# Query groups of 8, 10, 10, 10 and 10 rows in place of six of 8, with the key stacks in a ring of three thirds

## The chip, the cores and the metric

The kernel runs on one core of a Trainium2 chip. The metric is the time of one execution on the device in microseconds (us), as the median of several runs. Before the change it is 2807.74 us, the median of 3 runs that took 2807.44 to 2809.26.

## The reference

The input is four images (B = 4) of 384 channels (C) and 48 x 48 = 2304 tokens (N). There are eight heads of 48 channels. Inputs and outputs are float32. Cut to what matters:

```python
local = depthwise_conv_7x7(x) * bn_scale + bn_shift        # per channel
q, k, v = split_heads(layernorm(x) @ qkv_w.T + qkv_b)       # layernorm over channels
q = q + split_heads(layernorm(local))
attn = softmax(q @ k.T * 48 ** -0.5)
out = x + (attn @ v) @ proj_w.T + proj_b
```

So each image has two kinds of work: a convolution of 49 taps on each of 384 channels, which feeds the queries only, and attention of 2304 queries over 2304 keys in each of eight heads.

## The kernel before

**Tiling.** Channels lie on the 128 partitions in three chunks (`CC = 3`); tokens lie along the free dimension. An image is cut into `NG = 6` groups of `RG = 8` rows, that is `G = 384` columns. The same groups serve the queries, the keys, the values and the output projection. `NT = B * NG = 24` query groups are numbered `t = (b, g)`. Keys come in `KB = 18` blocks of 128. The eight heads form `NP = 4` pairs, and the two heads of a pair take the two halves of the partitions (the two row halves of the TensorE array).

**A slot.** The work of one query group is 12 slots (`NSLOT`): pair `s // 3`, and a third of the keys `s % 3`, which is `BATCH = 6` key blocks. Slot `s` first computes scores for its six blocks (`score_batch`, then `score`), and then weighs the values with them (`weigh_batch`, then `weigh`). For each block, `score` issues six matmuls with weights of 64 x 128 and 384 columns: three terms (high and low parts of queries and keys, stacked in `qs` and `ks`) times two row halves, in `float32r`, which takes one pass. They go to the two banks of a PSUM tile. One exponential on ScalarE takes the 768 columns to a tile `pt` in SBUF (a ring of 5 buffers). `weigh` issues two float32 matmuls per block, with weights of 128 x 64, one per head; each runs as two passes on the array, so that the profile counts four records. The 64 columns of a head's weights are its 48 values, a column of ones that sums the softmax's denominator, and 15 columns whose sums aren't read. At the end of the slot `sums_out` copies the sums out on ScalarE, and `sums_add` adds thirds on VectorE. The exponential is taken without subtracting a maximum first; `inside` keeps a flag of whether the denominators stayed in a safe range, and a second pass that subtracts it runs only if they did not, which the data here never ask for.

**Stacks of keys.** For an image, the stacks of all four pairs are written to DRAM (`wide`) by many small transfers in the keys' stage (`keys_out`, on GpSimd's queue, called POOL in the profile). Pair 0's is built in SBUF (through `stack_head` on SyncE's queue, SP) and kept in DRAM by `keep_stack` (one store of 2304 KB in slot 1 of the image's first group). During attention the pairs alternate in two SBUF buffers of a whole pair (tag `ks`, `bufs=2`). In each slot, `load_keys` issues the load of a third (768 KB) of the next pair.

**The convolution.** VectorE does it for group `t + 1` while TensorE works on group `t`: one `scalar_tensor_tensor` per tap and chunk (line 289), with a first `tensor_scalar` (285). For group 0 and group 1 some taps of chunk 0 (`PE_TAPS = 10` and `MORE_TAPS = 18`) run on TensorE, with diagonal weights (`products`). `load_slab` brings the rows of a group with three more on each side.

**What sets the order.** On TensorE, VectorE and ScalarE the instructions run in the order in which they are written. SP's and POOL's are placed by the framework's scheduler. Where convolution instructions go is decided by `plan`: each point of the program (two per slot, five per step of the keys' stage) has a `spare` time, each group's convolution a due point, and `convolve` takes the share of a point from one stream. In image 0 (`early`) the norm of the next group's local queries goes through TensorE: `mean_kept` multiplies by a matrix of means, first at slot `norm_slots(t)[0]`, which is 8 for group 0 and 7 for the others, and again a slot later. Then `centre`, `local_end` and `query_end` form the queries, and `high_queries` (ScalarE) and `low_queries` (VectorE, then small transfers within `qs` on SP) their stack. In later images these norms go through transfers instead (`following`).

**Between images** stands a keys' stage of six steps. Each step projects values, keys and queries of a group of the new image, and the output of a group of the old image (`fetch` of the attention held in DRAM, `load_residual`, `finish`); each is three matmuls of 384 columns per chunk (line 529, two passes each). The last group's output is not held, but read from SBUF.

```python
            score_batch(t, s)
            if s == 0:
                gather_tails(*reversed(queries[t]))
            if pair < NP - 1 or g < NG - 1:
                load_keys(b, (pair + 1) % NP, third)
            if s == 1 and g == 0:
                keep_stack(b)
```

Of the kernel before, what the change touches and what calls it, by code (L numbers as in the profile page):

```python
# [23 lines left out]
RG = 8  # L24
BATCH = 6
# [21 lines left out]
def unshifted_pass(  # L47
# [28 lines left out]
    NT = B * NG  # L76
    PAD = KS // 2

# [18 lines left out]

    xn = {}

    def place_x(b, g):  # L100
        xn[b, g] = big.tile([P, CC, G], F32, tag=f"xn{g}", name=f"xn{b}_{g}")
        return xn[b, g]
# [6 lines left out]
    def load_slab(b, g, parts=1, queue=nc.gpsimd):  # L109
        first, end = max(0, g * RG - PAD), min(H, (g + 1) * RG + PAD)  # L110
        t = work.tile([P, CC, (RG + 2 * PAD) * W], F32, tag="slab", name=f"slab{b}_{g}")

        edges = (first, (g + 1) * RG, end) if parts == 2 else (first, end)
        for a, e in zip(edges, edges[1:]):
            load_packed(t[:, :, (a - first) * W : (e - first) * W], x[b, :, a * W : e * W], queue)
        slabs[b, g] = (t, first, end)
# [11 lines left out]
    natural = work.tile([P, G], F32, tag="qt", name="natural", bufs=1)[:, 0 : CC * (T0 + 1)]  # L128
# [21 lines left out]
    start_up = big.tile([P, 2, N], F32, tag="ks", name="start_up", bufs=2).rearrange("p a n -> p (a n)")  # L150
# [58 lines left out]
    def pack():  # L209
# [19 lines left out]
        work.tile([P, 2, C], F32, tag="pt", name="pt", bufs=5) for _ in range(-(-PE_TAPS // 6))  # L229
    ]  # L230
    staged = [piece(CC, C) for _ in range(3)]
# [18 lines left out]
    def window(slab, a, g, first, end, c, tap):  # L250

        dy, dx = tap // KS - PAD, tap % KS - PAD
        r0, r1 = max(g * RG, -dy), min((g + 1) * RG, H - dy)
        c0, c1 = max(0, -dx), min(W, W - dx)
        if r0 >= r1:
            return None
        img = slab[:, c, : (end - first) * W].rearrange("p (h w) -> p h w", w=W)
        a = a.rearrange("p (h w) -> p h w", w=W)
        return (
            img[:, r0 + dy - first : r1 + dy - first, c0 + dx : c1 + dx],  # L260
            a[:, r0 - g * RG : r1 - g * RG, c0:c1],
        )

    def conv_ops(t):
        b, g = divmod(t, NG)
        if t + 1 < NT:
            load_slab(*divmod(t + 1, NG))
        slab, first, end = slabs[b, g]
        acc = work.tile([P, CC, G], F32, tag="acc", name=f"acc{t}", bufs=3)
# [29 lines left out]
    def products(g, n, diagonal):  # L299
        total = two_banks()[:, 0, :G]  # L300
# [11 lines left out]
    def make_more():  # L312
        for tag, bufs in (("qs", 5), ("qs", 5)):
            d = work.tile([P, CC, G], F32, tag=tag, name="more", bufs=bufs)
# [9 lines left out]
    def norm_slots(t):  # L324
        return (8 - (t > 0), None) if t + 1 < NG else (5, 8)

    def spare(t, s, half):
        b, g = divmod(t, NG)
        first, second = norm_slots(t)
        time = 3.6 - (0.0 if half else 0.6) - (0.6 if half and s % 3 == 1 else 0.0)  # L330
        if b + 1 < B and g >= later(b + 1):
# [5 lines left out]
        if t + 1 < NG:  # L337
# [3 lines left out]
        elif g < NG - 1:  # L341
# [3 lines left out]
        return max(0.3, time)  # L345

    def later(b):

        return X_LATER + (b == 1)

# [12 lines left out]
    for t in range(NT):  # L363
        if t % NG == 0 and t:
            points += [("kv", t, g, h) for g in range(NG) for h in range(5)]
            room += [spare_at_keys(t // NG, g, h) for g in range(NG) for h in range(5)]
# [3 lines left out]
    due = []  # L370
    for t in range(1, NT):
        last = ("slot", t - 1, norm_slots(t - 1)[0] - (t >= NG), t < NG) if t % NG else ("kv", t, 4, 0)
        due.append((points.index(last), t * each - MORE_TAPS))
    share = {}

    def plan(done):

        done = float(done)
        given = round(done)
        for i, point in enumerate(points):  # L380
            ahead = [(sum(room[i:end]), n - done) for end, n in due if end > i]
            rate = max((n / time for time, n in ahead[: 2 * NG]), default=0.0)
            done += rate * room[i]
            share[point] = round(done) - given
            given = round(done)
# [6 lines left out]
    few = G // 32  # L392

    def spread(s):

        return s.rearrange("p (k i) -> p k i", i=1).to_broadcast([P, few, 32])

    class Norm:
# [8 lines left out]
        def __init__(self, src):  # L407
            self.src = src
            self.buf = work.tile([P, CC, G], F32, tag="sq", name="sq")

        def squares(self, at=slice(0, G)):
# [20 lines left out]
        def mean(self, m=None):  # L432
            self.m = two_banks()[:, 0, :G] if m is None else m
            nc.tensor.matmul(self.m, lhsT=mean_w, rhs=self.buf[:, 0, :], start=True, stop=True)

        def mean_by_chunk(self, src, m=None):
            self.m = two_banks()[:, 0, :G] if m is None else m
            project(self.m, lambda c: mean_w, lambda c: src[:, c, :])

        def mean_kept(self, src):  # L440

            m = two_banks()[:, 0, :G]
# [9 lines left out]
        def centre(self, raw=None, at=slice(0, G)):  # L452
# [5 lines left out]
        def root(self, at=slice(0, G)):  # L458
# [6 lines left out]
        def newton(self, at=slice(0, G)):  # L465
# [7 lines left out]
        def out(self):  # L473

            part = work.tile([P, few], F32, tag="part", name="part")
            parts = dram.tile([32, 4, few], F32, tag="parts", name="parts")
            self.four = work.tile([P, 4 * few], F32, tag="four", name="four")
# [12 lines left out]
        def few_in(self):  # L490
            self.v = work.tile([P, few], F32, tag="few", name="few")
            nc.vector.tensor_reduce(
                self.v, self.four.rearrange("p (q k) -> p k q", k=few), AX.X, ALU.add
# [14 lines left out]
        def few_root(self):  # L508
            self.y = work.tile([P, few], F32, tag="few_y", name="few_y")
            self.u = work.tile([P, few], F32, tag="few_u", name="few_u")  # L510
# [11 lines left out]
        def scale(self, rs, at=slice(0, G)):  # L522
# [16 lines left out]
    values = {}  # L539
    lows = deque()  # L540
# [3 lines left out]
    def place_keys(b, p):  # L544
        stacks[b, p] = big.tile([P, 2, N], HALF, tag="ks", name=f"ks{b}_{p}", bufs=2)
        return stacks[b, p].bitcast(F32)
# [9 lines left out]
    def keys_out(b, g, u, k):  # L556
        at = slice(g * G, (g + 1) * G)
        k = k.bitcast(F32)
        if g == u == 0:
            place_keys(b, 0)  # L560
            for p in range(1, NP):
                wide[b, p] = dram.tile([P, 2, N], F32, tag=f"wide{p}", name=f"wide{b}_{p}")
        for j in range(2):
            if u == 0:
                stack_head(stacks[b, 0].bitcast(F32)[:, :, at], j, k, nc.sync)
# [12 lines left out]
    def keep_stack(b):  # L578
        wide[b, 0] = dram.tile([P, 2, N], F32, tag="wide0", name=f"wide{b}_0")
        nc.gpsimd.dma_start(out=wide[b, 0], in_=stacks[b, 0].bitcast(F32))  # L580

    def load_keys(b, p, i):
        at = slice(i * BATCH * P, (i + 1) * BATCH * P)
        if i == 0:
            place_keys(b, p)
        nc.gpsimd.dma_start(out=stacks[b, p].bitcast(F32)[:, :, at], in_=wide[b, p][:, :, at])  # L586

    def from_x(b, g, before=None, ao=None):
# [3 lines left out]
        flat = big.tile([P, NB * NH * HA + 64 - HA], F32, tag=f"v{g}", name=f"v{b}_{g}")  # L592
        v = flat[:, 0 : NB * NH * HA].rearrange("p (t h d) -> p t h d", t=NB, h=NH)
        values[b, g] = flat
        nc.gpsimd.memset(v[:, :, :, HD:HA], 1.0)
        nc.gpsimd.memset(flat[:, NB * NH * HA :], 0.0)
# [12 lines left out]
        def key(u, r):  # L609
# [3 lines left out]
            k = work.tile([P, 2, G], HALF, tag="pt", name=f"k{b}_{g}_{u}", bufs=5)  # L613
# [22 lines left out]
        def output(co, r):  # L636
            project(r[:, :G], lambda c: w_o[:, c, co * P : (co + 1) * P], lambda c: ao[:, c, :])
            yield
            finish(before, co, r[:, :G])
# [28 lines left out]
    row = work.tile([P, CC, G], F32, tag="rb", name="row", bufs=1)[:, 0]  # L668
# [85 lines left out]
    def query_end(t):  # L754

        acc = accs.pop(t)
        q = xn[divmod(t, NG)]
        q3 = work.tile([P, G], F32, tag="qt", name=f"qt{t}", bufs=1)
# [12 lines left out]
    def high_queries(t, p):  # L771
        qs = work.tile([P, 3, G], HALF, tag="qs", name=f"qs{t}_{p}", bufs=5)
# [22 lines left out]
    def sums_out():  # L795
# [3 lines left out]
        t, p, i, sums = ended.pop()  # L799
        if i:  # L800
            part = work.tile([P, G], F32, tag="part_o", name=f"o{t}_{p}_{i}")
            nc.scalar.copy(part[0 : 64 + HA], sums[0 : 64 + HA, 0, :G])  # L802
            parts_of.append((t, p, i, part))
            return
        if p == 0:
            ao = work.tile([P, CC, G], F32, tag="ao", name=f"ao{t}")
            ao3 = work.tile([P, G], F32, tag="aot", name=f"aot{t}", bufs=1)
            den = dram.tile([NH, G], F32, tag="den", name=f"den{t}")
# [3 lines left out]
        nc.scalar.copy(dst[0 : 64 + HA], sums[0 : 64 + HA, 0, :G])  # L812
# [21 lines left out]
    def divide(t):  # L834

        few = NH * G // P
        rd = work.tile([P, few], F32, tag="rd", name="rd")
        rb = work.tile([P, CC, G], F32, tag="rb", name="rb", bufs=1)
        rden = dram.tile([NH, G], F32, tag="rden", name=f"rden{t}")
# [3 lines left out]
        for bound, op in ((SAFE, ALU.is_le), (1 / SAFE, ALU.is_ge)):  # L843
            nc.vector.scalar_tensor_tensor(inside, rd, bound, inside, op, ALU.mult)
        nc.sync.dma_start(out=rden.rearrange("h (k f) -> (h k) f", f=few), in_=rd)
        heads = rden[0:6].rearrange("(c h) n -> h c n", h=2)
        for j in range(2):
# [3 lines left out]
                out=rb[r : r + HD], in_=heads[j : j + 1].to_broadcast([HD, CC, G])  # L851
            )
            nc.sync.dma_start(out=rb[r + HD : r + 64], in_=last.to_broadcast([16, CC, G]))
# [4 lines left out]
    def load_residual(t, tag="qs", bufs=5):  # L858
        b, g = divmod(t, NG)
        xr = work.tile([P, CC, G], F32, tag=tag, name=f"xr{t}", bufs=bufs)  # L860
        nc.gpsimd.dma_start(
            out=xr, in_=x[b, :, g * G : (g + 1) * G].rearrange("(c p) n -> p c n", p=P)
        )
        residuals[t] = xr
# [3 lines left out]
    def hold(t):  # L868
        held[t] = dram.tile([P, CC, G], F32, tag=f"held{t % NG}", name=f"held{t}", bufs=1)
        nc.gpsimd.dma_start(out=held[t], in_=outputs[t][0])  # L870

    def fetch(t):
        if t < NT - NG:
            ao = work.tile([P, CC, G], F32, tag="qs", name=f"af{t}", bufs=5)
        else:
            ao = big.tile([P, CC, G], F32, tag=f"xn{t % NG}", name=f"af{t}")
# [903 lines left out]
```

## Time and profile before

| | |
|---|---|
| median of 3 runs | 2807.74 us (2807.44 to 2809.26) |
| the profiled execution | 2808.18 us |
| its span in the profile | 2806.1 us |
| what lies around the span | 2.1 us |
| granted TensorE clock, mean | 0.995 of full speed |
| attention of image 0 starts at | 169.8 us |
| a query group's 12 slots, mostly | 88.3 us |
| query groups 0, 1, 2 of image 0 | 93.7, 100.2, 93.7 us |
| keys' stages between images | 144.5, 143.5, 140.1 us |
| the last slot ends at | 2765 us |

The engines are PE (TensorE's matmuls), PEld (its loads of weights), DVE (VectorE), ACT (ScalarE), POOL (GpSimd) and SP (SyncE). A profiled line of a group of instructions names the line in the kernel, the engine, the operation, output <- inputs, and the shapes. In the windows view each engine has its busy time and, in brackets, its number of instructions; then come the granted clock, the busy share of the DMA engines and what they moved in GB/s. A busy time says how much an engine had to do, not whether anyone waited for it: for that the chain of work that ended last and the waits are read.

### The profile page before, as it was taken

Reading aid. Unit: us, or ns where it says so; the run is one execution under the profiler, and the core shown is the slowest. Engines: PE = TensorE matmul, PEld = TensorE weight load, DVE = VectorE, ACT = ScalarE, POOL = GpSimd, SP = SyncE. Lnnn points to the kernel's source line nnn. Section 1 sums busy time; section 2 is a strip of 40 time slices with the busy share of each in tenths; the row PEclk is TensorE's granted clock in tenths of the full one; section 3 lists DMA queues with packets and bytes.
Section 4 is the critical chain, followed back from the end, with each engine's and each line's share of the span. In section 5 each row is a group of like instructions: output and inputs, shape, how many; then the busy total and the mean of one; then the engine's idle time right before and its main releaser. Section 6 shows DMA issues by size and latency. Waiting matters only on the chain.

```text
span 2806.1 us, 53985 instructions
## 1 busy us (share of the span) xinstructions
PE 2773.0 (99%) x19330; PEld 1747.7 (62%) x19330; DVE 2430.9 (87%) x4801; ACT 1648.4 (59%) x2659; POOL 729.7 (26%) x1353
## 2 busy tenths in 40 slices
PE   9999999999999999999999999999999999999999
PEld 6565666666655666666655566666665566666665
DVE  6879999988999999999888999998988999998402
ACT  4356666667424766677632566777662266666762
POOL 5731111111374111111156311111117711111110
PEclk9999999999999999999999999999999999999999
DMA  7354545455455455545545544455445554554542
GB/s 139 98 143 131 154 136 147 146 157 161 105 155 164 127 161 146 159 154 166 156 118 146 171 144 151 142 167 173 138 122 148 142 167 147 155 175 152 170 143 72
DMA packets 180919, 410.35 MB, mean 146 GB/s; under 512 B 67776, under 2 KB 122240, under 8 KB 180128
## 3 DMA queue, kind: packets, MB, share of 16 engines
q0 software_dynamic: 84736, 325.45, 37.0%
q1 hardware_dynamic: 92912, 77.73, 12.0%
q8 instruction: 155, 2.54, 0.4%
q10 hardware_dynamic: 2992, 3.62, 0.4%
q14 instruction: 124, 1.02, 0.1%
HBM read 298.25 MB, written 64.73 MB: 129 GB/s over the span
## 4 chain that ended last, share of the span: by engine, by line
PE 87%; DVE 6%; DMA 3%; POOL 1%; issue 1%; ACT 1%; SPq 0%; DVEq 0%; ACTq 0%; POOLq 0%
PE o L917 39%; PE r L902 33%; PE r L529 14%; DVE acc L289 3%; DMA qs<-qs 1%; PE r L304 1%; DMA parts<-part 1%; DMA wide<-k 1%; POOL wide L554 0%; DMA four<-parts 0%; DVE k L617 0%; DMA ks<-k 0%; DMA rd<-den 0%; DVE xn L761 0%; DVE xr L883 0%
## 5 line engine op out<-in xcount | busy, mean ns | idle before, releaser
L289 DVE SCALAR_TENSOR_TENSOR acc<-slab,vec,acc 128x368 f32<-128x368 f32 (+7 forms) x3430 | 1762.5, 586 | 2.2
L910 ACT ACTIVATE pt<-r 128x768 f32<-128x768 f32 x1728 | 1247.8, 827 | 104.0 <-PE r L902 68.4
L917 PE MATMUL o<-pt,v 128*64 128x384 f32 x6912 | 1178.3, 490 | 0.0
L902 PEld LDWEIGHTS r<-qs,ks 64*128 64x128 f32 x10368 | 898.2, 186 | 197.2 <-issue 178.2
L902 PE MATMUL r<-qs,ks 64*128 64x384 f32 x10368 | 995.4, 341 | 20.3 <-DMA qs<-qs 9.1
L917 PEld LDWEIGHTS o<-pt,v 128*64 128x64 f32 x6912 | 470.9, 137 | 586.8 <-issue 507.2
L586 POOL DMA_DIRECT2D ks<-wide x276 | 200.1, 727 | 1025.6 <-PE r L902 976.4
L802 ACT COPY o<-o 113x384 f32<-113x384 f32 x192 | 92.4, 481 | 402.5 <-PE o L917 402.5
L529 PE MATMUL r<-xn,w_qk 128*128 128x384 f32 x864 | 283.7, 486 | 0.0
L529 PEld LDWEIGHTS r<-xn,w_qk 128*128 128x128 f32 x864 | 164.2, 190 | 114.5
L529 PE MATMUL r<-w_v,xn 128*128 128x384 f32 x432 | 144.9, 488 | 0.0
L606 ACT COPY v<-r 128x384 f32<-128x384 f32 x72 | 32.1, 481 | 186.9 <-PE r L529 186.9
L821 DVE TENSOR_TENSOR ao<-ao,o 113x384 f32<-113x384 f32 x144 | 79.8, 554 | 66.9 <-ACT o L802 66.3
L529 PE MATMUL r<-af,w_o 128*128 128x384 f32 x360 | 119.1, 487 | 0.0
L529 PEld LDWEIGHTS r<-w_v,xn 128*128 128x128 f32 x432 | 81.4, 190 | 58.6 <-issue 2.4
L812 ACT COPY ao<-o 113x384 f32<-113x384 f32 x72 | 34.6, 481 | 139.7 <-PE o L917 139.7
L95 POOL DMA_DIRECT2D slab<-in_x_dram x92 | 55.6, 613 | 222.6 <-DVE acc L289 216.7
L529 PEld LDWEIGHTS r<-af,w_o 128*128 128x128 f32 x360 | 68.2, 190 | 47.8 <-issue 0.6
L554 POOL DMA_DIRECT2D wide<-k x192 | 96.3, 506 | 5.4 <-issue 5.0
L95 POOL DMA_DIRECT2D xn<-in_x_dram x72 | 39.5, 557 | 212.5 <-DVE qs L779 212.5
L576 POOL DMA_DIRECT2D wide<-k x192 | 92.7, 488 | 6.8 <-issue 2.6
L570 POOL DMA_DIRECT2D wide<-k x144 | 71.1, 496 | 83.1 <-ACT k L614 61.3
(136 smaller groups left out, 1302.1 us busy)
## 6 DMA issues: line engine op xcount, KB each, us to landing
ks<-wide POOLq DMA_DIRECT2D x276, 768.0 KB, 6.5
qs<-qs SPq DMA_DIRECT2D x528, 48.0 KB
xr<-in_x_dram POOLq DMA_DIRECT2D x24, 576.0 KB, 5.8
slab<-in_x_dram POOLq DMA_DIRECT2D x32, 378.0 KB, 6.6
wide<-k POOLq DMA_DIRECT2D x480, 24.0 KB, 1.9
held<-ao POOLq DMA_DIRECT2D x20, 576.0 KB, 3.3
af<-held POOLq DMA_DIRECT2D x20, 576.0 KB, 5.1
rb<-rden SPq DMA_DIRECT2D x48, 216.0 KB
```

The source lines that it names most:

```text
L95: queue.dma_start(out=dst[p0 : p0 + piece.shape[0]], in_=piece)
L289: nc.vector.scalar_tensor_tensor(dst, src, weight, dst, ALU.mult, ALU.add)
L529: nc.tensor.matmul(dst, lhsT=weights(c), rhs=src(c), start=c == 0, stop=c == CC - 1)
L554: queue.dma_start(out=dst[r + 32 * i : r + 32 * i + 32, 1], in_=k[r + 16 : r + HD, 1])
L570: nc.gpsimd.dma_start(out=last[16 * u : 16 * u + 16, 0], in_=k[r : r + 16, 0])
L576: nc.gpsimd.dma_start(out=last[to : to + 16, 1], in_=k[r : r + 16, 1])
L586: nc.gpsimd.dma_start(out=stacks[b, p].bitcast(F32)[:, :, at], in_=wide[b, p][:, :, at])
L802: nc.scalar.copy(part[0 : 64 + HA], sums[0 : 64 + HA, 0, :G])
L821: nc.vector.tensor_add(dst, dst, part[0 : 64 + HA])
L902: nc.tensor.matmul(r[:, j, :G], lhsT=ks[rows, w, kb * P : (kb + 1) * P], rhs=qs[rows, m, :], start=i == 0, stop=i == 2,)
L910: nc.scalar.activation(pt, r[:, :, :G], AF.Exp, scale=SCALE)
L917: nc.tensor.matmul(sums[halves[j], 0, :G], lhsT=values[t // NG, kb // NB][:, first : first + 64], rhs=pt[:, j, :], start=i == 0, stop=i == ...
```

## The change

The rows of an image are cut twice. The queries, their convolution and norms go in five groups, of 8, 10, 10, 10 and 10 rows (`ROWS`, `NA = 5`), which is one of 384 columns and four of 480 (`GM`); `NT` becomes 20, and `tokens[g]` is a group's slice of the columns. Keys, values and the projections of the keys' stage stay in six groups of 384 columns. The output projection has pieces of its own (`pieces_out`): four of 384, one of 288 and one of 480 columns, of which the last is the last query group.

What follows from it in the buffers:

- x lies in one SBUF tile (`whole`) instead of six, the values in one (`every_value`) instead of six, and the held attention of an image in one DRAM tile. Groups are slices of these.
- The key stacks lie in a ring of three buffers that each have a third of a pair, instead of two that have a whole pair. `load_keys(b, n)` loads the third of slot `n = s + 2`, one per slot. `keep_stack` stores thirds, the first two in the keys' stage (steps 3 and 5), the third in slot 0.
- `pt` has 4 buffers instead of 5. Tiles of a query group are made for 480 columns (`qs`, `acc`, `sq`, `ao` and so on). The weights that are prepared at the start lie in `qs` tiles meanwhile.
- `plan` weighs the convolution by columns. Norms, `divide` and DRAM tiles take the size of their group. `begins(b)` is the query group in which the next image's x starts to be normalized.

The diff, cut to its core:

```diff
+ROWS = 8, 10, 10, 10, 10
...
+    NA = len(ROWS)
+    NT = B * NA
+    GM = max(ROWS) * W
+    row_of = [sum(ROWS[:g]) for g in range(NA + 1)]
+    tokens = [slice(row_of[g] * W, row_of[g + 1] * W) for g in range(NA)]
+    pieces_out = [slice(i * G, min((i + 1) * G, tokens[-1].start)) for i in range(NG - 1)]
+    pieces_out.append(tokens[-1])
...
+    whole = big.tile([P, CC, N], F32, tag="xn", name="xn")
...
-        xn[b, g] = big.tile([P, CC, G], F32, tag=f"xn{g}", name=f"xn{b}_{g}")
+        xn[b, g] = whole[:, :, g * G : (g + 1) * G]
...
-        return max(0.3, time)
+        return max(0.3, time) * columns_of(t) / G
...
+    def begins(b):
+
+        return NA - NG + later(b)
...
-        last = ("slot", t - 1, norm_slots(t - 1)[0] - (t >= NG), t < NG) if t % NG else ("kv", t, 4, 0)
-        due.append((points.index(last), t * each - MORE_TAPS))
+        last = ("slot", t - 1, norm_slots(t - 1)[0] - (t >= NA), t < NA) if t % NA else ("kv", t, 4, 0)
+        counts.append(t * each - MORE_TAPS)
+        weights.append(weights[-1] + (counts[-1] - counts[-2]) * columns_of(t) / G)
+        due.append((points.index(last), weights[-1]))
...
+    every_value = big.tile([P, KB * NH * HA + 64 - HA], F32, tag="v", name="v")
...
-    def place_keys(b, p):
-        stacks[b, p] = big.tile([P, 2, N], HALF, tag="ks", name=f"ks{b}_{p}", bufs=2)
-        return stacks[b, p].bitcast(F32)
+    def place_keys(b, p, i):
+        stacks[b, p, i] = big.tile([P, 2, third], HALF, tag="ks", name=f"ks{b}_{p}_{i}", bufs=3)
+        return stacks[b, p, i].bitcast(F32)
...
-    def keep_stack(b):
-        wide[b, 0] = dram.tile([P, 2, N], F32, tag="wide0", name=f"wide{b}_0")
-        nc.gpsimd.dma_start(out=wide[b, 0], in_=stacks[b, 0].bitcast(F32))
-
-    def load_keys(b, p, i):
-        at = slice(i * BATCH * P, (i + 1) * BATCH * P)
-        if i == 0:
-            place_keys(b, p)
-        nc.gpsimd.dma_start(out=stacks[b, p].bitcast(F32)[:, :, at], in_=wide[b, p][:, :, at])
+    def keep_stack(b, i):
+        at = slice(i * third, (i + 1) * third)
+        nc.gpsimd.dma_start(out=wide[b, 0][:, :, at], in_=stacks[b, 0, i].bitcast(F32))
+
+    def load_keys(b, n):
+        p, i = n // 3 % NP, n % 3
+        at = slice(i * third, (i + 1) * third)
+        nc.gpsimd.dma_start(out=place_keys(b, p, i), in_=wide[b, p][:, :, at])
...
         def output(co, r):
-            project(r[:, :G], lambda c: w_o[:, c, co * P : (co + 1) * P], lambda c: ao[:, c, :])
+            n = ao.shape[-1]
+            project(r[:, :n], lambda c: w_o[:, c, co * P : (co + 1) * P], lambda c: ao[:, c, :])
...
-        qs = work.tile([P, 3, G], HALF, tag="qs", name=f"qs{t}_{p}", bufs=5)
+        qs = work.tile([P, 3, GM], HALF, tag="qs", name=f"qs{t}_{p}", bufs=5)
+        qs = qs[:, :, : columns_of(t)]
...
     def score(t, p, kb):
-        ks, qs = stacks[t // NG, p], stacked[t, p]
+        ks, qs = stacks[t // NA, p, kb // BATCH], stacked[t, p]
+        at = slice(kb % BATCH * P, (kb % BATCH + 1) * P)
+        n = columns_of(t)
...
-                    r[:, j, :G],
-                    lhsT=ks[rows, w, kb * P : (kb + 1) * P],
+                    r[:, j, :n],
+                    lhsT=ks[rows, w, at],
...
-        pt = work.tile([P, 2, G], F32, tag="pt", name="pt", bufs=5)
-        nc.scalar.activation(pt, r[:, :, :G], AF.Exp, scale=SCALE)
+        pt = work.tile([P, 2, GM], F32, tag="pt", name="pt", bufs=4)[:, :, :n]
+        nc.scalar.activation(pt, r[:, :, :n], AF.Exp, scale=SCALE)
...
+        if g in (3, 5):
+            keep_stack(0, g // 2 - 1)
...
+                if gk in (3, 5):
+                    keep_stack(b, gk // 2 - 1)
...
-            if pair < NP - 1 or g < NG - 1:
-                load_keys(b, (pair + 1) % NP, third)
-            if s == 1 and g == 0:
-                keep_stack(b)
+            if s == 0 and g == 0:
+                keep_stack(b, 2)
+            if (s or g) and (s < NSLOT - 2 or g < NA - 1):
+                load_keys(b, s + 2)
```

## The prediction

> **What bounds the kernel now.** I read three views in this order: busy times, the chain that ended last, the timeline of one slot. The page first:
>
> ```profile
> PE 2773.0 (99%) x19330; PEld 1747.7 (62%) x19330; DVE 2430.9 (87%) x4801; ACT 1648.4 (59%) x2659; POOL 729.7 (26%) x1353
> ...
> PE 87%; DVE 6%; DMA 3%; POOL 1%; issue 1%; ACT 1%; SPq 0%; DVEq 0%; ACTq 0%; POOLq 0%
> ```
>
> TensorE is busy 99% and carries 87% of the chain, so the change is worth what it does to PE's instruction stream, unless another engine starts to hold PE up. The candidate is VectorE: 87% is a mean, and some stages are fuller. The timeline of PE in one slot (start, length, ..., count):
>
> ```profile
> 2411.89 3.41 PE L902 MATMUL r<-qs,ks 64*128 64x384 f32 x36
> 2415.23 4.09 PE L917 MATMUL o<-pt,v 128*64 128x384 f32 x24
> 2419.25 0.97 PE L902 MATMUL r<-qs,ks 64*128 64x384 f32 x8
> ```
>
> A slot is 36 score matmuls, then 24 records of weighing; the next starts at 2419.25, so it lasts 7.36 us. Between starts the trace shows 173.4 ns for two scores (the two row halves run side by side) and 322.5 ns for a pass of weighing over both column halves. 18 x 173.4 + 12 x 322.5 = 6991 ns; the other 367 ns are the seams: +108 before the first score, +112 from score to weigh, +50 at the first weigh, +97 back. Twelve slots make 88.3 us, and most groups take 88.3.
>
> Groups 0 to 4 of image 0 are longer, because there PE computes the next group's norm means and needs its convolution finished. By stage (core 0: PE, PEld, DVE, ACT, POOL busy):
>
> ```profile
> 169.80:263.50 93.70, 92.96 (x734) 58.64 (x733) 82.81 (x154) 62.98 (x96) 14.99 (x24) 1.00 0.49 147
> 263.50:363.70 100.20, 95.35 (x736) 60.50 (x734) 92.38 (x179) 63.07 (x96) 14.00 (x21) 0.98 0.48 140
> 363.70:457.40 93.70, 92.95 (x736) 58.64 (x734) 91.20 (x177) 62.64 (x96) 14.05 (x21) 1.00 0.50 145
> ```
>
> DVE is at 91.20 of 93.70 in the third. In the first it was idle for 9.77 us at the start (to 178.16, behind ACT's copy of qs) and then ran without a gap:
>
> ```profile
> 227.78 7.61 DVE L289 SCALAR_TENSOR_TENSOR acc<-slab,vec,acc 128x376 f32<-128x376 f32 x12
> 235.31 0.47 DVE L285 TENSOR_SCALAR acc<-slab,vec 128x384 f32<-128x384 f32 x1
> 235.96 2.20 PE L529 MATMUL r<-acc,mean_w 128*128 128x384 f32 x6
> ```
>
> conv(1) ends at about 235.3, and PE comes to its mean at 235.96: 0.7 us of slack. This is where larger groups will hurt.
>
> **What the Trainium skill says.** "TensorE: Matmul & The Clock Gate", section "Back-to-back issue gap", gives N/2.4 + 2.5 ns for a single matmul. Two column halves of 384 make 322.5, as the trace has it; for scores it would be 162.5, the trace has 173.4, so their extra 10.9 ns follows another rule. The same page, "LDWEIGHTS (loading the stationary operand)", gives P/1.2: 107 ns for 128 columns and 53 for 64; the seams of 108 and 50 agree. A seam costs one exposed weight load, whatever the columns. "PSUM — Partial Sum Buffer", "The four PSUM rules": one output may have 512 fp32 columns; 480 fits, but no run here shows it yet. "VectorE: DVE Perf Modes", "The TRN2 errata — SBUF-src ops pay a fixed extra latency per instruction", says a cost fixed per instruction: convolution starts are 364 ns apart at 225 columns and 529 at 384, that is 129 ns + 1.04 per column.
>
> **The change, part by part.**
>
> *Slots of 480 columns.* Each interval grows by 96/2.4 = 40 ns per column half: scores 213.4 (the 13.4 beyond 160 kept), weighing 402.5, seams unchanged. 18 x 213.4 + 12 x 402.5 + 367 = 9038 ns, against 1.25 x 7358 = 9198 for the same columns. An image goes from 6 x 88.3 = 529.8 to 88.3 + 4 x 108.46 = 522.1 us; four images: **-30.6**. Of it -17.6 is 48 slots' seams, -11.6 are scores, -1.4 weighing. Extra columns in an existing instruction were never seen, so I bound the scores: strictly proportional (216.7 ns) gives back 11.6; if the 10.9 ns stand for weight loads that 480 columns cover, a pair takes 202.9 and 3456 pairs gain 10.5 ns each, 36 more.
>
> *Norm means on PE in image 0*: five times +5.45 become four times two means of 6 x 402.5 ns and 1.6 of waits, 6.4: **-1.6**.
>
> *Products of group 1*: 18 taps x 2 passes x 92 columns x 0.83 ns = **+2.8**.
>
> *VectorE in group 0.* Group 0 keeps 384 columns, so PE arrives at the mean as early as before, while conv(1) now has 480. After the gap at 178 there are 98 of its instructions, each 0.096 to 0.10 us longer: 9.4 to 9.8 us. Slack was 0.7, so PE waits about **+9** in slot 8 (conv ops move with the planner's weights, but the due point is the same). In group 1 PE lost 6.35 us in the first slot to late qs transfers. If that recurs, DVE catches up and the net is +9.4; if it goes, DVE is 3.5 short at the next mean, net +6.5. I take **+8**. Later DVE gains: its instruction grows by 629/529 = 1.19 while PE's group grows by 1.23 to 1.25, 3430 convolution instructions become 2854.
>
> *Ring of three thirds.* 276 key loads become 228, issued one per slot instead of three per pair. A load waits for the scores of the slot before, and has two slots and most of a score phase, 2 x 9.04 + 5 = 23 us, to land:
>
> ```profile
> ks<-wide POOLq DMA_DIRECT2D x276, 768.0 KB, 6.5
> ```
>
> "DMA: Bandwidth & Descriptors", "Anatomy of one DMA", would give 2.0 + 786/436 = 3.8 us as an estimate; the trace's 6.5 decides. So 16 us of cover: 0. SP issues 440 qs loads for 528, in the same slots. It also breaks up bursts: in group 8 one slot took 12.01 us because three loads released together ran ahead of a qs transfer, so I take **-3** (0 to -4.65). The keep of pair 0 becomes three stores, two of them in the keys' stage on POOL's queue before stack pieces: 8 more issues of 0.56 us; POOL has about 15.7 of 23 us per step there, so 0, at worst +3.4 over three boundaries.
>
> *Image boundaries.* PE idles about 5 us there for the first qs. The output projection now has 288 columns in the fifth and 480 in the last piece, so the last query chain starts 1.44 us earlier under the same PE work: up to -4.3 for three, **-2** taken. Tail +0.4.
>
> *pt ring 5 to 4.* The fifth and sixth exp of a slot now wait for its first two weighings. At 0.85 us each (0.691 now), the sixth ends 7.0 us into the slot and is needed at 8.1: covered by 1.1 us; if not, every slot would lengthen. One tile for x and one for values: waits go by region in the changed program, 0. One held tile per image, read in pieces that straddle groups: each fetch follows its stores by whole groups, 0.
>
> Sum: -30.6 - 1.6 + 2.8 + 8 - 3 - 2 + 0.4 = **-26**. The profiled execution took 2808.18 (span 2806.1 and 2.1 around it), 0.4 above the median of 2807.74. That gives **2782**, with the terms' bounds 2773 to 2796.
>
> **Rivals.**
>
> *Scores proportional to columns* (12%): no seam inside, +11.6, 2794. Against it stands 322.5 = 2 x 160 + 2.5 for weighing, where the constant is small.
>
> *Scores set by weight loads* (9%): the slot is 8.85 us or less, about 2746. For it: each pair needs two loads of 128 columns, and weighing, with loads of 64, has no such extra. Against: short matmuls with one such load each start 112 ns apart, far under 173.4, and the two row halves' loads overlap.
>
> *VectorE bounds more of image 0* (10%): if the planner's shares put convolution later in groups 1 to 3 too, three more waits of 5 to 6 us: 2800. For it: 91.20 of 93.70. Against: DVE's 1.19 against PE's 1.23.
>
> *The ring comes late* (9%, the slower side). POOL issues in order, and behind a wait every key load is held:
>
> ```profile
> POOL ks L586 <- PE r L902: 976.4, 77, 26.3
> POOL slab L95 <- DVE acc L289: 216.7, 19, 24.6
> POOL xn L95 <- DVE qs L779: 212.5, 18, 18.1
> ```
>
> (total, times, longest, us.) A wait of 24.6 that begins just after a load holds the next one 24.6 - 9.0, then come 2.2 of slab issues and 6.5 to land: 24.3, 1.3 beyond the 23. With 37 x 20/24 = 31 such waits it decides from 26/31 = 0.84 us each; at 1.3 each the time is 2822. Against it: the waits before mostly end before the loads behind them are due, since they start with the burst; a single load per slot lets them sit closer to their release.
>
> That the change doesn't do what it says is unlikely: instruction counts of the changed program are 8640 scores and 2880 weighings against 10368 and 3456.
>
> **The numbers.** Likeliest case 60%: 2782. A measurement tells 0.2% (5.6 us) from no change: faster is under 2802.1, slower over 2813.4. Cases below: main, proportional, weight loads and most of VectorE: 0.84 faster; rest of VectorE and mild ring delays 0.07; ring 0.09. The range reaches from between the main case and the weight-load case, 2764, to the VectorE case, 2802.
>
> **What will show it.** Slots of 9.04 us (9.20: proportional; 8.85: weight loads); score pairs 213 ns apart; in group 0 about 9 us of PE idle ahead of the mean, released by DVE's convolution; key loads landed before their scores, no wait of PE on ks; a smaller share of DVE later. It would be wrong if PE's waits on ks or pt appear in many slots, or if DVE's waits go beyond group 1.

## The result and the profile after

The changed kernel takes 2783.61 us (median of 4 runs, 2782.53 to 2784.88) against 2808.50 for the kernel before (4 runs): a ratio of 0.991, with a 95% interval of 0.9893 to 0.9927. That is faster by 24.9 us; the prediction was 2782. The profiled execution took 2782.53 us with a span of 2780.7, which is 25.4 us less than the span before.

The page of the changed kernel, busy times and the chain by engine:

```profile
PE 2749.9 (99%) x16438; PEld 1555.9 (56%) x16438; DVE 2339.9 (84%) x4082; ACT 1639.0 (59%) x2281; POOL 696.2 (25%) x1273
...
PE 87%; DVE 5%; POOL 4%; DMA 2%; issue 1%; ACT 1%; SPq 0%; DVEq 0%; ACTq 0%; POOLq 0%
```

PE still sets the time (99% busy, 87% of the chain), with 23 us less of busy time. DVE's share fell from 87 to 84%. One slot of 480 columns in the timeline of PE (start, length, line, form, count):

```profile
2413.57 4.16 PE L952 MATMUL r<-qs,ks 64*128 64x480 f32 x36
2417.66 5.05 PE L967 MATMUL o<-pt,v 128*64 128x480 f32 x24
2422.64 0.70 PE L952 MATMUL r<-qs,ks 64*128 64x480 f32 x4
```

From 2413.57 to 2422.64 are 9.07 us. The first three query groups of image 0, in the windows view (length, then busy PE, PEld, DVE, ACT and POOL, granted clock, DMA share, GB/s):

```profile
171.50:278.00 106.50, 97.20 (x733) 59.61 (x732) 91.44 (x146) 64.91 (x96) 13.29 (x20) 0.95 0.43 121
278.00:396.40 118.40, 115.29 (x736) 61.38 (x734) 116.07 (x190) 77.27 (x96) 14.31 (x21) 1.00 0.43 123
396.40:511.80 115.40, 114.68 (x736) 61.37 (x734) 109.92 (x181) 77.35 (x96) 14.28 (x21) 1.00 0.45 124
```

Group 0 has the 384 columns it had before, yet takes 106.5 us instead of 93.7. PE is busy for only 97.20 of it, and its clock is 0.95. The timelines of VectorE and PE around the mean show why:

```profile
237.03 9.51 DVE L307 SCALAR_TENSOR_TENSOR acc<-slab,vec,acc 128x480 f32<-128x480 f32 x13
246.46 0.55 DVE L868 TENSOR_TENSOR ao<-ao,o 113x384 f32<-113x384 f32 x1
```

```profile
234.80 4.09 PE L967 MATMUL o<-pt,v 128*64 128x384 f32 x24
246.69 5.14 PE L568 MATMUL r<-acc,mean_w 128*128 128x480 f32 x6 [7.80 <-DVE acc L307]
```

VectorE works without a gap until the convolution of group 1 ends at about 246.5; PE is done with its slot at 238.9 and waits 7.80 us. The six matmuls that follow take 5.14 us, where the same six take 2.68 in the next group (at 353.63).

From the two traces, stage by stage, the 25.4 us are made up as follows (after minus before, us):

| part | predicted | found |
|---|---|---|
| slots: 192 of 9.075 and 48 of 7.378, for 288 of 7.357 | -30.6 | -22.3 |
| norm means on PE in image 0: 4 x 6.4 for 5 x 5.45 | -1.6 | -1.6 |
| products of group 1, start of the attention 169.8 to 171.5 | +2.8 | +1.7 |
| VectorE and the qs wait in groups 0 and 1 | +8 | +8.2 |
| group 8's long slot | -3 | -4.65 |
| three image boundaries | -2 | -6.0 |
| tail | +0.4 | -0.7 |
| sum | -26 | -25.35 |

The sum agrees with the span, so nothing large is missing. The slots brought 8.3 us less than predicted, and the boundaries, group 8, the start and the tail together 7.8 us more.

### The profile page after: what moved, and what is told of

It is laid out like the page before. It is cut to its first block, busy times and chain, and to the rows that moved or that the text cites. A ratio compares the mean times of both kernels' runs of the same rounds, so it can differ in the third digit from the quotient of the medians.

```text
span 2780.7 us, 46399 instructions
## 1 busy us (share of the span) xinstructions
PE 2749.9 (99%) x16438; PEld 1555.9 (56%) x16438; DVE 2339.9 (84%) x4082; ACT 1639.0 (59%) x2281; POOL 696.2 (25%) x1273
## 3 DMA queue, kind: packets, MB, share of 16 engines
q1 hardware_dynamic: 83072, 77.72, 12.2%
## 4 chain that ended last, share of the span: by engine, by line
PE 87%; DVE 5%; POOL 4%; DMA 2%; issue 1%; ACT 1%; SPq 0%; DVEq 0%; ACTq 0%; POOLq 0%
PE o L967 40%; PE r L952 32%; PE r L568 14%; DVE acc L307 4%; POOL wide L594 1%; DMA wide<-k 1%; DMA slab<-in_x_dram 1%; POOL wide L619 1%; POOL wide L592 1%; POOL wide L591 0%; POOL wide L613 0%; DVE k L661 0%; PE r L322 0%; DMA qs<-qs 0%; PE r L1010 0%
## 5 line engine op out<-in xcount | busy, mean ns | idle before, releaser
L307 DVE SCALAR_TENSOR_TENSOR acc<-slab,vec,acc 128x450 f32<-128x450 f32 (+8 forms) x2854 | 1679.8, 657 | 2.2
L960 ACT ACTIVATE pt<-r 128x960 f32<-128x960 f32 (+1 forms) x1440 | 1248.4, 943 | 236.4 <-PE o L967 148.9
L967 PE MATMUL o<-pt,v 128*64 128x480 f32 (+1 forms) x5760 | 1167.9, 555 | 4.1 <-ACT pt L960 4.1
L952 PE MATMUL r<-qs,ks 64*128 64x480 f32 (+1 forms) x8640 | 970.9, 374 | 9.5 <-DMA qs<-qs 6.3
L952 PEld LDWEIGHTS r<-qs,ks 64*128 64x128 f32 x8640 | 784.9, 184 | 277.6 <-issue 168.2
L967 PEld LDWEIGHTS o<-pt,v 128*64 128x64 f32 x5760 | 393.1, 137 | 663.7 <-issue 581.7
L849 ACT COPY o<-o 113x480 f32<-113x480 f32 (+1 forms) x160 | 87.1, 544 | 299.4 <-PE o L967 299.4
L868 DVE TENSOR_TENSOR ao<-ao,o 113x480 f32<-113x480 f32 (+1 forms) x120 | 76.1, 634 | 96.1 <-ACT o L849 96.0
L568 PE MATMUL r<-af,w_o 128*128 128x384 f32 (+1 forms) x270 | 85.2, 470 | 0.0
L675 ACT ACTIVATE xn<-r,qkb 128x384 f32<-128x384 f32 x72 | 41.0, 578 | 64.7 <-PE r L568 63.1
```

The costliest lines, as they stand in the source:

```text
L307: nc.vector.scalar_tensor_tensor(dst, src, weight, dst, ALU.mult, ALU.add)
L568: nc.tensor.matmul(dst, lhsT=weights(c), rhs=src(c), start=c == 0, stop=c == CC - 1)
L849: nc.scalar.copy(part[0 : 64 + HA], sums[0 : 64 + HA, 0, :n])
L868: nc.vector.tensor_add(dst, dst, part[0 : 64 + HA])
L952: nc.tensor.matmul(r[:, j, :n], lhsT=ks[rows, w, at], rhs=qs[rows, m, :], start=i == 0, stop=i == 2,)
L960: nc.scalar.activation(pt, r[:, :, :n], AF.Exp, scale=SCALE)
```

## The experiments

### The buffers and the order, without the larger groups

```diff
-ROWS = 8, 10, 10, 10, 10
+ROWS = 8, 8, 8, 8, 8, 8
```

> The changed kernel with ROWS = 8, 8, 8, 8, 8, 8: every buffer and order of the change, but query groups of 384 columns. Theory (the columns carry the gain, the buffers only mend waits at the image boundaries, in group 8 and in group 1): no wait of 10 us in group 0, boundaries 6 us shorter, group 8 4.65 shorter, group 1 about 3 shorter, slots of 7.36 to 7.375; 2795 to 2800 us. Rival (the buffers and the ring carry all of it): about 2784. Rival (only the columns matter): 2808. Score pairs: 173.4 ns apart if the wider pair of the changed kernel comes from its rows padded to 480 columns, 176 if it comes from the ring or the pt buffers.

2824.63 us (5 runs), a ratio of 1.0056 to the kernel before, interval 1.0041 to 1.0071: **slower by 16.7 us**. The theory, the rival of 2784 and that of 2808 all fell. So the larger groups are worth about 41 us (2824.6 to 2783.6), and what came with them, taken alone, costs. The wait for VectorE in group 0 is gone, and the boundaries between images are 2.2 us shorter than before. But slots take 7.388 us instead of 7.357, which makes 8.9 us in 288, and single slots inside groups 1 to 3 and 7 to 16 are longer than usual by 21.5 us in all, where the kernel before had 11 in groups 1 and 8. Behind that are waits of PE, and a lower clock after some of them (last section). The largest sum of waits in the whole trace (what PE waited for, total, times, longest):

```profile
PE r L952 <- DMA qs<-qs: 16.1, 14, 4.2
```

These are the small transfers that build the stack of queries. The longest shows how: SP's queue stands from 1188.96 to 1195.95 between storing partial sums of a norm and fetching them, with key and x loads issued by POOL at 1189.13 and 1189.85, and the qs transfers of the next pair, whose low part VectorE finished at 1187.15, are behind it.

```profile
1188.96 0.56 SPq L520 DMA_DIRECT2D parts<-part  x1
1195.95 0.55 SPq L521 DMA_DIRECT2D four<-parts  x1
1196.61 0.58 SPq L832 DMA_DIRECT2D qs<-qs  x1
```

The same with tiles padded to 480 columns:

```diff
-    GM = max(ROWS) * W
+    GM = 10 * W
```

> As r8x6 (groups of 384 columns), but the tiles are made for 480 columns as in the changed kernel. Theory (a cost that comes with the stride of the padded rows, about 2.6 ns per score pair): pairs at 176 ns here and at 173.4 in r8x6. Rival (ring or pt buffers): the same interval in both.

One run: 2818.53 us. Score pairs stand 175.8 ns apart here and 176.0 in r8x6, so the padding doesn't widen them.

The same as r8x6, but without the loads of keys, so that three pairs of four are scored with the keys of pair 0:

```diff
     def load_keys(b, n):
         p, i = n // 3 % NP, n % 3
         at = slice(i * third, (i + 1) * third)
-        nc.gpsimd.dma_start(out=place_keys(b, p, i), in_=wide[b, p][:, :, at])
+        stacks[b, p, i] = stacks[b, 0, i]
```

> r8x6 (all of the change but the larger groups) without its loads of key thirds, as in no_key_loads (three pairs of four get wrong keys). r8x6 lost some 21 us to waits of PE for qs transfers inside groups 1 to 3 and 7 to 13. Theory (a load per slot runs beside the small transfers of the qs stack and of the norms, and a slot of 7.4 us leaves them no room): most of these waits go, 2800 to 2808 us. Rival (VectorE or the x transfers make them late, the loads play no part): 2818 us or more.

2808.72 us (12 runs), 15.9 less than r8x6; 0.7 above the band of the theory. Every wait for qs of more than 0.5 us inside groups 1 to 3 and 7 to 16 is gone, the step from store to fetch of a norm's sums takes 2.0 us (1188.41 to 1190.42 on SP's queue), and of the qs waits this is left:

```profile
PE r L952 <- DMA qs<-qs: 2.3, 4, 0.8
```

The band was missed because about 8 us came back at the boundaries before the third and fourth image (152.5 us from the last slot's start instead of 148.7, and a first slot of 14.45 instead of 10.36). So a key load in every slot does get in the way of the small transfers, and at 7.4 us per slot there is no room for that. Whether it does so in the DMA engines or in POOL's queue is not separated: the run also takes away POOL's waits ahead of each load, so that its other transfers are issued earlier. At 9.07 us there is room: in the changed kernel such waits inside a group are left in two slots of image 0 only, 3.0 us in group 1's first slot and 0.85 in slot 6 of group 0.

### The ring alone, and the smaller pt ring alone, on the kernel before

```diff
-        stacks[b, p] = big.tile([P, 2, N], HALF, tag="ks", name=f"ks{b}_{p}", bufs=2)
+        stacks[b, p, i] = big.tile([P, 2, third], HALF, tag="ks", name=f"ks{b}_{p}_{i}", bufs=3)
...
-            if pair < NP - 1 or g < NG - 1:
-                load_keys(b, (pair + 1) % NP, third)
-            if s == 1 and g == 0:
-                keep_stack(b)
+            if s == 0 and g == 0:
+                keep_stack(b, 2)
+            if (s or g) and (s < NSLOT - 2 or g < NG - 1):
+                load_keys(b, s + 2)
```

> The kernel before with the ring of three thirds alone (one load per slot, three keeps, two of them in the keys' stage; the weights at the start lie in a tile of their own). Theory (the ring breaks up the bursts): group 8's slot of 12.0 us becomes 7.4 (-4.65), the first slot of group 1 shrinks by 3 to 6; with the boundaries unchanged 2799 to 2802 us; if the shorter boundaries come from the ring too, 2793 to 2796. Rival (no part of the ring): 2808, or slower, if its loads come late. Score pairs 176 ns if the ring is what widened them, 173.4 if not.

2809.21 us (12 runs), ratio 1.0005 (0.9996 to 1.0013): as the rival said, no gain. The ring did what was said of it, since group 8's slot of 12.01 is 8.91 and group 1's first slot 9.88 instead of 13.69. It gave that back in slot 6 of groups 2, 3 and 10 (8.36, 11.48, 8.73), in group 9, and in 0.02 us on each slot (7.376). That is the length of the changed kernel's slots of 384 columns (7.378), though the pairs are not wider by their first scores (173.3 ns): here the second score of a pair falls behind the first, and the first weighing comes 128 ns beyond the pair instead of 102.

So the ring alone leaves 15.4 us of r8x6 unexplained (2824.6 against 2809.2). About 9 of it are more waits for small transfers (21.5 against 13), about 3.5 longer slots. Of the other changes only the smaller pt ring was run alone:

```diff
-        pt = work.tile([P, 2, G], F32, tag="pt", name="pt", bufs=5)
+        pt = work.tile([P, 2, G], F32, tag="pt", name="pt", bufs=4)
```

(and the same for keys and diagonals.)

> The kernel before with 4 pt buffers instead of 5. Theory (the exp ring has slack inside a slot, and matters only at the start of an image, where its buffers still hold keys): slots of 7.355 as before, each image's first slot 0.5 to 1.5 us longer, 2808 to 2812 us. Rival (the smaller ring is what makes the changed kernel with six groups of 8 rows 15 us slower than the ring of thirds alone): 2818 us or more.

2808.56 us (20 runs), ratio 1.0003 (0.9996 to 1.001), slots of 7.356: no effect at 384 columns. The first slots of images didn't grow as expected (10.42, 10.39 and 10.51 us for 10.35, 11.15 and 10.45). The profiled execution is the slowest of the 20 (2819.87 us): its attention starts 6.2 us later, and slot 6 takes 11.50 us in group 7 and 15.17 in group 10. The 20 executions lie between 2805.45 and 2819.87, so what is read from this one trace is only the length of an ordinary slot.

### VectorE in group 0

```diff
...
     plan(n_first - (each - PE_TAPS))
+    ahead = 16
+    share["slot", 0, 0, 0] += ahead
+    for s in range(7, 1, -1):
+        for h in (1, 0):
+            cut = min(ahead, share["slot", 0, s, h], 2)
+            share["slot", 0, s, h] -= cut
+            ahead -= cut
...
```

> The changed kernel with 16 convolution instructions of group 1 moved from slots 2 to 7 of group 0 to its first point, where VectorE stands idle for 10 us. Theory (the wait of 10.6 us at the mean in slot 8 of group 0 is VectorE's convolution, which the idle stretch can take): the wait falls by 8 to 10.6 us, slot 8 from 20.3 to 10 to 12 us, 2773 to 2776 us. Rival (the stretch isn't free, since the queries' low parts or the slab come later and give the time back): slot 8 stays near 20, or slot 1 or 2 grows, 2783 us.

2771.87 us (4 runs), ratio to the kernel before 0.9869 (0.9852 to 0.9886), 11.7 less than the changed kernel, 1.1 below the expected band, and the best version found. Slot 8 of group 0 takes 9.99 us instead of 20.31; the first slot of group 1 grew from 12.07 to 13.49, which is the lower clock after its wait (last section). VectorE's timeline shows the moved instructions fill the stretch in which it stood for 9.98 us (37 instead of 21 in one run, then 0.23 us of idle time):

```profile
156.92 22.74 DVE L307 SCALAR_TENSOR_TENSOR acc<-slab,vec,acc 128x450 f32<-128x450 f32 x37
179.88 0.56 DVE L825 TENSOR_TENSOR qs<-xn,qs 128x384 fp32r<-128x384 f32 x1 [0.23 <-ACT qs L820]
```

Two runs took away the wait that stands next, in group 1's first slot. One starts the qs stack of group 1 earlier:

```diff
...
                 query_end(t + 1)
+                if t == 0:
+                    high_queries(t + 1, 0)
...
+            if t == 0 and s == first + 2:
+                low_queries(t + 1, 0)
             convolve("slot", t, s, 1)
```

(The calls at the old place, a slot later, are left out for group 0.)

> front16, and in group 0 the first query stack of group 1 is begun right after its queries are done (one slot earlier in program order on ScalarE and VectorE). Theory (after front16 PE's longest wait in image 0 is 2.4 us for the qs transfers of group 1's first slot, and the lower clock that follows it costs about 2 us more): first slot of group 1 from 13.5 to 9.1 to 10.5 us, 2767.5 to 2769.5 us. Rival (the transfers are late because key loads run beside them, not because they start late): first slot still over 12, 2771 to 2772 us.

2772.82 us (4 runs): no gain over front16. The first slot of group 1 is 9.08, as the theory said, which is 4.4 us less. But slots 6 and 7 became 10.48 and 13.31 instead of 9.07 and 11.69, 3.0 us together: 1.4 of it stand at a wait for qs in slot 6, 1.6 at VectorE's convolution ahead of the mean. The rest went elsewhere: the attention starts 1.5 us later, and the first slots of the third and fourth image changed by +1.7 and -1.9. The other run leaves out the key loads of the changed kernel (the edit of r8x6_no_key_loads):

> The changed kernel without its 228 loads of key thirds: every pair is scored with the stacks of pair 0 that lie in the ring (so three pairs of four get wrong keys), everything else is done. Theory (the loads into the ring run beside the scores and widen their pairs by 3 ns): pairs at 213.4 ns instead of 216.7, slots of 9.04; with fewer transfers beside qs, group 1's first slot nearer 9.1 than 12.1; 2771 to 2776 us. Rival (the ring's loads are fully hidden and touch nothing): pairs at 216.7, 2782 to 2784 us.

2789.39 us (4 runs), which is 5.8 more than with the loads, outside the bands of theory and rival; 5.3 of it are longer boundaries. Slots stay at 9.075 and pairs at 216.5, as the rival said. Group 1's first slot is 9.09; then PE waits for VectorE twice instead of once:

```profile
PE r L568 <- DVE acc L307: 10.7, 2, 8.7
```

The second wait, 2.0 us, makes slot 7 of group 1 15.22 instead of 11.69, so 3.5 with the lower clock after it. So in groups 0 and 1 VectorE is the bound: of a wait of PE that is taken away before its mean, a part returns at the mean, 1.6 us in one run and 3.5 in the other. The prediction had put that at 3.5.

### The order of the groups

```diff
-ROWS = 8, 10, 10, 10, 10
+ROWS = 10, 10, 10, 10, 8
```

> The changed kernel with ROWS = 10, 10, 10, 10, 8: the group of 384 columns comes last, and the output projection has six pieces of 384. Theory (VectorE's wait comes from a convolution of 480 columns beside a group of 384, and the boundaries gained from the last output piece of 480): no wait at the mean in group 0 (-10.6), 4 us back at the three boundaries, at most 13 us more ahead of the attention for the larger first convolution: 2777 to 2791 us. Rival (the wait comes with image 0 whatever the order of the groups): still about 10 us at the mean of group 0 or 1, over 2787 us.

2778.74 us (4 runs). No wait for VectorE is left in the attention; the attention starts at 185.3 instead of 171.5, 13.8 later. The boundaries didn't get longer by 4 us: beyond their 139.5 us of PE work each and the slots' own length they take 12.2 us in all, against 13.4 in the changed kernel.

```diff
-ROWS = 8, 10, 10, 10, 10
+ROWS = 10, 8, 10, 10, 10
```

> The changed kernel with ROWS = 10, 8, 10, 10, 10. Theory: no wait at the mean in group 0 (-10.6); group 1 now stands where group 0 stood, but VectorE can run ahead in group 0, so its wait is under 5 us; boundaries as in the changed kernel; 0 to 13 us more ahead of the attention: 2773 to 2790 us. Rival (the wait moves to group 1 in full): 2784 to 2797 us.

2776.05 us (4 runs). No wait in group 0 or 1, and the start is 5.2 us later (176.7). Both kernels confirm that the wait comes from a convolution of 480 columns beside a group of 384 that VectorE has not run ahead of.

### What a score pair costs

```diff
...
-        stacks[b, p, i] = big.tile([P, 2, third], HALF, tag="ks", name=f"ks{b}_{p}_{i}", bufs=3)
+        if not ring:
+            ring.append(big.tile([P, 2, N], HALF, tag="ks", name="ks"))
+        stacks[b, p, i] = ring[0][:, :, i * third : (i + 1) * third]
```

> The changed kernel with the three thirds of the key ring side by side in one tile of 2304 columns, so that high and low parts of a key lie 9216 bytes apart as before the change, not 3072. Theory (the layout of the stacks widened the score pairs by 3 ns): pairs 213.4 ns apart instead of 216.7, slots of 9.04 instead of 9.07, 2776 to 2778 us. Rival (the layout plays no part): pairs at 216.7, 2783 to 2785 us.

2784.08 us (4 runs), pairs at 216.5 ns: that the thirds lie in three tiles plays no part.

```diff
-ROWS = 8, 10, 10, 10, 10
+ROWS = 8, 10, 8, 6, 8, 8
```

> The changed kernel with ROWS = 8, 10, 8, 6, 8, 8, so that slots of 480, 384 and 288 columns stand in one execution. Score pairs at 480, 384 and 288 columns: fixed cost and columns (16 + N/2.4): 216, 176 and 136 ns; proportional to columns: 216, 173 and 130; bound by their weight loads below some size: 216, 176 and well over 136. Slots of 288 columns with seams of 0.34 us: 18 x 136 + 12 x 242.5 + 340 = 5.7 us (fixed), 5.6 (proportional).

One run: 2847.4 us. In one execution the pairs stand 134.3, 175.7 and 216.3 ns apart at 288, 384 and 480 columns. That is 0.43 ns per column and 11 ns fixed: between the two laws, nearer to the fixed one, and no floor from weight loads. The slots take 5.67, 7.38 and 9.07 us. Here three slots of 288 columns in PE's timeline:

```profile
2571.64 2.69 PE L952 MATMUL r<-qs,ks 64*128 64x288 f32 x36
...
2577.33 2.68 PE L952 MATMUL r<-qs,ks 64*128 64x288 f32 x36
...
2582.99 2.68 PE L952 MATMUL r<-qs,ks 64*128 64x288 f32 x36
```

Short slots are also where the waits sit: slot 6 of groups 3, 9 and 15 (288 columns) takes 9.25, 7.71 and 9.47 us.

## Why the prediction was right, point by point

**The bound** was read rightly: PE's stream sets the time, and seams saved are the gain. Fewer seams stayed the largest term of the sum.

**The slot of 480 columns** was mis-sized: 9.075 us, not 9.038. Weighing measured exactly what was predicted (402.5 ns). Score pairs did not: 216.5 ns instead of 213.4. The step that failed is "the 13.4 beyond 160 kept": in every kernel with all of the change's buffers the pairs are wider at 384 too (175.7 to 176.0 for 173.7), with a part of it won back at the seam to weighing, which shrank from 102 ns beyond the pair to 88 (92 at 480 columns; of 38 ns per slot at 384 that is 14). 192 slots x 0.037 and 48 x 0.02 give 8.1 of the 8.3 us missed. That 216.5 is 1.25 times 173.4 looks like the rival of proportional cost, but the row of three sizes shows it isn't that law. What widened the pairs stays open. It was not the padding, not the three tiles of the ring, not its transfers and not the pt ring. The ring alone made slots as long (before_ring) without widening the first scores' interval; where the other tiles lie was not tested.

**VectorE in group 0** was right in place and cause, and near in size: about 9 predicted. PE waited 7.8, and then lost another 2.5 to a lower clock, which the prediction didn't have; slot 6 lost 0.85 to a qs wait. Of the 6.35 us that the first slot of group 1 lost before (4.1 of waiting, 1.7 at a lower clock), 3.0 are left. The net is 8.2 for 8, within the bounds of 6.5 and 9.4, but a smaller wait and a clock that was not counted make it up.

**The ring** was half right. "So 16 us of cover: 0" holds for the loads' own landing: no view has a wait of PE on ks, and pairs and slots are the same without the loads. What the prediction left out is what a load in every slot does to others, the transfers of qs and of the norms. At 384 columns the ring gives back what it mends (before_ring: 1.0005). With the larger groups 3.9 us of such waits are left.

**Group 8** gained 4.65, the upper bound given, but breaking up bursts is not enough for it: at 384 columns a single load per slot leaves waits there too (8.91 us for that slot in before_ring, 9.20 in r8x6). In the longer slots none is left. Of the 4.65 before, 2.4 were the wait and 1.6 the lower clock after it.

**The boundaries** gained 6.0 where 2 was taken and 4.3 was the bound. The step "the last query chain starts 1.44 us earlier" failed: with a last piece of 384 (rows_10_10_10_10_8) the boundaries were no longer. "PE idles about 5 us there" was true of the first boundary only: ahead of an image's first scores PE waited 4.9, 2.5 and 0.5 us before the change. The first slots of the three images show another part. Before, then after (length, busy PE, granted clock, DMA share, GB/s):

```profile
877.67:888.02 10.35, 9.95 (x60) 0.74 0.51 169
1558.69:1569.84 11.15, 10.56 (x61) 0.69 0.50 134
2232.27:2242.72 10.45, 9.32 (x61) 0.84 0.49 140
```

```profile
875.49:886.79 11.30, 8.32 (x61) 1.00 0.59 156
1543.03:1554.50 11.47, 9.71 (x61) 0.85 0.57 152
2210.83:2223.55 12.72, 9.83 (x63) 0.87 0.61 177
```

What the clock lacks to 1.00, times the length, is 2.7, 3.5 and 1.7 us before and 0, 1.7 and 1.7 after. So, as an estimate, about 4 of the 6 us are work that no longer ran at the lower clock. What shortened or moved the waits ahead of it was not isolated. The boundaries also moved by several us with nothing but transfers left out (13.4 us beyond PE's work in the changed kernel, about 19 without key loads), so a part of these 6 us may be luck of the order.

**The pt ring.** "Covered by 1.1 us" holds in ordinary slots: none is longer for it. PE waited for pt ahead of a weighing three times, 4.1 us in all, each in an image's first slot. Ahead of the first of them the exponential itself had waited 1.80 us (to 881.83) for transfers of keys out of `pt` buffers. The traces of the kernel before and of before_pt4 have no such wait, so the smaller ring alone doesn't make it.

**The rivals.** Weight loads as the bound: refuted, since a pair of 288 columns takes 134.3. VectorE as a bound in groups 1 to 3: no wait of PE for it there in the changed kernel. The ring late: no load is late at 480 columns; POOL's longest wait ahead of it fell from 24.6 to 18.3:

```profile
POOL slab L108 <- DVE acc L307: 153.4, 15, 18.3
```

That the sum came out 1.6 us from the result rests on two errors of 8 us with opposite signs, which is luck. The slots and group 8 came out within the bounds stated for them, the boundaries did not. The forecast that the change is faster, and that fewer and larger slots bring most of it, did not rest on that luck.

## What to carry to other kernels

A seam that costs the same whatever the size is worth removing by larger tiles. Here it is 0.34 to 0.35 us per slot at 288, 384 and 480 columns (what is left of the slots of rows_8_10_8_6_8_8 after 18 pairs and 12 passes of weighing). Longer steps also widen the cover of every small transfer that has one step to land: slots lengthened by such waits cost 21.5 us in r8x6 and 3.9 in the changed kernel, about as much as the 17.6 that the prediction gave to the seams, and only the run with all of the change but the size showed it. Where one group is smaller than the next, compare each engine's work for the next group with the time of the present one; the stretch in which the bounding engine stands idle just before is the place to put the excess. In a stage bounded by a second engine, much of a wait that is taken from the first comes back where it next needs the second.

## What the runs showed of the hardware

A wait of PE costs more than itself. After the 7.80 us in group 0 the granted clock was 0.50 for 5.1 us, in the windows view of the changed kernel (granted clock third from the end):

```profile
238.80:246.60 7.80, 0.09 (x2) 0.00 (x0) 7.45 (x12) 0.48 (x1) 0.00 (x0) 0.68 0.02 6
246.60:249.00 2.40, 2.31 (x3) 1.18 (x4) 2.40 (x6) 0.00 (x0) 2.16 (x4) 0.50 0.35 59
249.00:251.70 2.70, 2.70 (x4) 0.67 (x2) 2.70 (x5) 0.00 (x0) 0.90 (x2) 0.50 1.05 192
```

Passes took 0.80 us instead of 0.40, about 2.5 us more. The Trainium skill has this ("TensorE: Matmul & The Clock Gate", section "What's actually happening": half the clock after an idle window of about 3.4 us), and this wait agrees. But in front16 a shorter one was enough. After 2.4 us of waiting in group 1's first slot, 35 score matmuls took 5.73 us, where 36 usually take 4.16:

```profile
270.25:273.66 3.41, 3.41 (x20) 0.50 0.02 5
```

Nor does the length of a wait decide alone: the changed kernel has a wait of 2.4 us in the same slot, and its clock in the 3.5 us from 281.00 on was 1.00. That is why this slot took 12.07 us there and 13.49 in front16. What decides which of two such waits is followed by the lower clock is not shown here.
